# The state operand of a chunked scan, scaled on ScalarE in eight copies in place of one GpSimd product

## The chip, the cores and the metric

The kernel runs on one core of a Trainium2 chip. The metric is the device time of one execution in microseconds (us). The core has five engines that run side by side and meet at semaphores: TensorE (PE in the profile, with its weight loads as PEld), VectorE (DVE), ScalarE (ACT), GpSimd (POOL) and SyncE (SP), which issues the transfers. Each engine takes its own instructions strictly in order.

## The reference

One layer of a Mamba-2 block and a LoRA mixture stand side by side on the same normalised input, and both are added to it. Cut to what matters (L = 2048 positions, 64 heads of width 64, 8 groups of heads, state width 128):

```python
xn = layernorm(x)
proj = xn @ in_proj_w.T                 # gate, (x, B, C) and dt
xBC = silu(causal_conv4(proj[xBC]))
dt_p = softplus(dt + dt_bias); dA = exp(dt_p * -exp(A_log))
def step(state, inp):                   # over the 2048 positions
    state = state * dA_t + (dt_p * x)_t * B_t
    y_t = state . C_t
y = group_norm(y + x * D) * norm_weight * silu(gate)
out = x + y @ out_proj_w.T + ffn(xn)    # ffn: base matmul + top-2 LoRA
```

## The kernel before, in words

All is in float32. The input projection, the output projection and the base matrix are multiplied by Strassen-Winograd schemes with seven products per two-by-two block. In the first part (to about 2690 us) the products of the input projection (`pair`, seven products of eight half-matmuls each) run as a stream of TensorE work, and the scan's small matmuls are set between them. In the last part only the output projection runs.

The step-by-step recurrence is computed in chunks of Q = 128 positions. There are 16 groups-by-halves per 1024 positions, of four chunks each, so 128 slots, one for each chunk of each group of HG = 8 heads. A slot has two halves in the code:

- `scan_a` prepares a chunk, one slot ahead of its use. VectorE's `tensor_tensor_scan` at L688 makes `es`, for each of 8 heads and each of 128 positions the product of decays from a source position to a later one; `es` has one buffer (pool `p1`). TensorE makes C times B and a transpose of B in `ps_cb`, which ScalarE copies out (`cbm` L698, `bt` L700); VectorE multiplies `es` by `cbm` into `dab` (L702). TensorE transposes x into `ps_xt` (L88); ScalarE copies it out head by head, each scaled by its dt, into `xdt` (L713, eight copies of 128x64). Then `xdd` is `xdt` times the decay from each position to the chunk's end, the last column of `es`. `xdd` has one buffer too.
- `scan_b` uses it: eight matmul pairs `ps_y` from `xdt` and `dab`, four pairs `ps_e` from the state and C, VectorE's `ecp` and `y` (L759, L760), then the matmul `ps_st` from `bt` and `xdd` (L764). The state is multiplied by the chunk's whole decay on GpSimd (L769, through the helper `gp`, L83) and `ps_st` is added on VectorE (L774).

What else stands on the engines around it: on GpSimd the sums of weights for the Strassen scheme (`add` in `left_operands`, L427, and `level_one_sums` for the output weights `wo`, through L83); on ScalarE the copy `s1` of product one (L474), stores' functions (L529, L533), the convolution's first tap (L640), its silu (L653), squares (L798) and the norm's root (L809); on VectorE the other taps of the convolution (L646) and the sums that read a product's PSUM (L478, L482, L531). The fourth product of the second PSUM tile (`px`) writes the bank that an L531 has to have read.

The order on each engine is made when the program is recorded: a scheduler places the instructions by its own costs, and those given to `keep_in_program_order` keep the order of the code (the matmuls through `mm`, the `xdt` copies, and GpSimd's products in the second half through `gp`). Transfers all go through SyncE's queue.

Of the kernel before, what the change touches and what calls it, by code (L numbers as in the profile page):

```python
# [9 lines left out]
AF = mybir.ActivationFunctionType  # L10
ALU = mybir.AluOpType
# [5 lines left out]
HP = 64  # L17
G = 8
HG = H // G
# [8 lines left out]
P = 128  # L28
# [3 lines left out]
Q = 128  # L32
# [10 lines left out]
def mamba_lora_kernel(  # L43
# [17 lines left out]
    nc = tc.nc  # L61
# [16 lines left out]
    def mm(*args, **kw):  # L78
        tc.keep_in_program_order(nc.tensor.matmul(*args, **kw))  # L79

    def gp(s, *args):

        ins = nc.gpsimd.tensor_tensor(*args)  # L83
        if s:
            tc.keep_in_program_order(ins)

    def transpose(out, in_):
        tc.keep_in_program_order(nc.tensor.transpose(out, in_, ident))  # L88
# [590 lines left out]
    def scan_a(s, g, half, c):  # L679

        key = s, g, half, c
        n = f"{s}_{g}_{half}_{c}"
        dab, ecp = decay_of.pop(key)
        hs = slice(g * HG, (g + 1) * HG)
        cs = slice(c * Q, (c + 1) * Q)

        es = p1.tile([P, HG, Q], F32, tag="es", name=f"es_{n}")
        nc.vector.tensor_tensor_scan(  # L688
            es.rearrange("p h t -> p (h t)"), dab.rearrange("p h t -> p (h t)"), here, 0.0,
            ALU.mult, ALU.add,  # L690
        )
        yield
        xg, bc = xbc_of[s, g, half]
        psm = ps_one.tile([P, 2, Q], F32, tag="aux", name=f"ps_cb_{n}")
        mm(psm[:, 0, :], bc[:, 0, cs], bc[:, 1, cs], start=True, stop=True)
        transpose(psm[:, 1, :], bc[:, 0, cs])
        cbm = p2.tile([P, Q], F32, tag="cbm", name=f"cbm_{n}")
        nc.scalar.copy(cbm, psm[:, 0, :])  # L698
        bt = p2.tile([P, Q], F32, tag="bt", name=f"bt_{n}")
        nc.scalar.copy(bt, psm[:, 1, :])  # L700
        ms = dab
        nc.vector.tensor_tensor(  # L702
            ms, es, cbm.unsqueeze(1).to_broadcast([P, HG, Q]), ALU.mult
        )
        yield
        pst = ps_one.tile([P, 4, Q], F32, tag="aux", name=f"ps_xt_{n}")
        for j in range(4):
            transpose(pst[:, j, :], xg[:, j, cs])
        xdt = p2.tile([P, HG, HP], F32, tag="xdt", name=f"xdt_{n}")
        x_t = pst.rearrange("p j (a q) -> p (j a) q", q=HP)  # L710
        for h in range(HG):
            at = g * HG + h
            ins = nc.scalar.activation(  # L713
                xdt[:, h, :], x_t[:, h, :], AF.Copy,
                scale=dt_of[s][:, half * NQ + c, at : at + 1],
            )
            tc.keep_in_program_order(ins)

        xdd = p1.tile([P, HG, HP], F32, tag="xdd", name=f"xdd_{n}")
        gp(s, xdd, xdt, es[:, :, Q - 1 : Q].to_broadcast([P, HG, HP]), ALU.mult)  # L720
        mid_of[key] = ms, ecp, bt, xdt, xdd
        yield

# [231 lines left out]
    for _ in scan_a(*blocks[0], 0):  # L955
        pass
# [17 lines left out]
    for b, blk in enumerate(blocks):  # L974
        s, g, half = blk
# [15 lines left out]
        for c in range(NQ):  # L991
# [22 lines left out]
            if b == 1 and c < 2:  # L1014
# [3 lines left out]
                    lambda j=j: nc.sync.dma_start(xop_d[0][j], ops_of["x", 0][j]) for j in js  # L1018
                ]
            a = scan_a(*follow) if follow else iter(())  # L1020
            parts = [side[i * len(side) // n : (i + 1) * len(side) // n] for i in range(n)]

# [376 lines left out]
```

## Time and profile before

| what | value |
|---|---|
| median of 3 runs | 3461.18 us (3456.09 to 3463.89) |
| the profiled execution's own time | 3459.94 us |
| its span | 3458.2 us |
| TensorE busy | 3409.4 us (99%) |
| VectorE busy | 2530.2 us (73%) |
| ScalarE busy | 926.4 us (27%) |
| GpSimd busy | 832.3 us (24%) |
| `xdd` on GpSimd, L83 | 128 instructions, 145.3 us busy |
| `xdt` on ScalarE, L713 | 1024 instructions, 223.2 us busy |

The span is the time from the first to the last instruction of the profiled execution. A group's row gives its busy time, the mean duration of one instruction in ns, and the idle time of its engine just before it with what ended that idle time. TensorE's granted clock is at 0.996 of full speed, so differences are not of the clock. From the start to 180 us the kernel normalises the input and makes the decays; from 180 to about 2690 us the slots run, some 19.7 us each; the rest is the output projection.

### The profile page before, as it was taken

How to read it: one execution, taken by the hardware profiler on the slowest of the kernel's cores; microseconds unless marked ns; L12 is line 12 of the kernel's file. 1: busy time of each engine (PE TensorE's matmuls, PEld its weight loads, DVE VectorE, ACT ScalarE, POOL GpSimd, SP SyncE). 2: the span in 40 equal slices, each digit the busy share in tenths (PEclk: the TensorE clock that was granted, in tenths of full speed). 3: DMA queues.
4: the chain of work that ended last, by engine and by line, in shares of the span. 5: the costliest groups of instructions: out<-in, count | busy, mean ns of one | idle time of the engine just before them, and what ended most of it. 6: DMA issues, size and time to landing. Idle time of an engine off the chain costs nothing.

```text
span 3458.2 us, 37638 instructions
## 1 busy us (share of the span) xinstructions
PE 3409.4 (99%) x12818; PEld 1993.4 (58%) x12818; DVE 2530.2 (73%) x2861; ACT 926.4 (27%) x2158; POOL 832.3 (24%) x571
## 2 busy tenths in 40 slices
PE   9999999999999999999999999999999999999999
PEld 7444544544545554444555555444445588888888
DVE  7548787877887877677888887777885466566665
ACT  2223343333433333323333333333331000000000
POOL 3133323233333211332332433322332000000000
PEclk9999999999999999999999999999999999999999
DMA  6546655655656676787787788787777687585644
GB/s 234 189 164 201 209 178 189 206 191 197 199 193 205 197 262 220 246 283 231 240 251 245 234 260 253 234 255 226 244 233 270 236 279 242 198 299 188 213 165 145
DMA packets 530319, 769.79 MB, mean 223 GB/s; under 512 B 35152, under 2 KB 264656, under 8 KB 527440
## 3 DMA queue, kind: packets, MB, share of 16 engines
q1 hardware_dynamic: 530128, 767.39, 68.6%
q8 instruction: 102, 1.67, 0.2%
q14 instruction: 89, 0.73, 0.1%
HBM read 516.64 MB, written 250.61 MB: 222 GB/s over the span
## 4 chain that ended last, share of the span: by engine, by line
PE 77%; DVE 10%; issue 6%; DMA 4%; POOL 2%; ACT 1%; SPq 0%; POOLq 0%; DVEq 0%; ACTq 0%
PE ps_x_x L79 10%; PE ps_x_w L79 8%; PE ps_a_x L79 7%; PE ps_y_x L79 7%; PE ps_x_g L79 6%; PE ps_a_w L79 6%; PE ps_y_w L79 6%; PE ps_y_g L79 4%; PE ps_a_g L79 4%; PE ps_y L79 3%; PE ps_e L79 3%; PE ps_x_b L79 2%; PE ps_st L79 2%; PE ps_a_b L79 2%; PE ps_y_b L79 2%
## 5 line engine op out<-in xcount | busy, mean ns | idle before, releaser
L688 DVE TENSOR_TENSOR_SCAN es<-dab,here 128x1024 f32<-128x1024 f32 x128 | 327.3, 2557 | 285.8 <-POOL xdd L83 264.6
L83 POOL TENSOR_TENSOR xdd<-xdt,es 128x512 f32<-128x512 f32 x128 | 145.3, 1135 | 1003.4 <-ACT xdt L713 967.6
L646 DVE SCALAR_TENSOR_TENSOR xg<-rawx,cw,xg 128x512 f32<-128x512 f32 x384 | 339.8, 934 | 22.3 <-ACT xg L640 21.7
L79 PE MATMUL ps_x_w<-t,w 128*128 128x256 f32 x1344 | 303.8, 379 | 0.0
L79 PEld LDWEIGHTS ps_x_w<-t,w 128*128 128x128 f32 x1344 | 255.4, 190 | 41.5 <-issue 7.7
L713 ACT ACTIVATE xdt<-ps_xt,dt 128x64 f32<-128x64 f32 x1024 | 223.2, 331 | 201.4 <-PE ps_xt L88 201.4
L83 POOL TENSOR_TENSOR wo<-wo 128x512 f32<-128x512 f32 (+1 forms) x112 | 214.1, 1912 | 16.6 <-DMA ecp<-run_d 10.3
L83 POOL TENSOR_TENSOR state<-state,tot 128x512 f32<-128x512 f32 x112 | 134.5, 1201 | 322.4 <-PE ps_e L79 311.0
L79 PE MATMUL ps_a_w<-q,w 128*128 128x256 f32 x896 | 202.5, 379 | 0.0
L702 DVE TENSOR_TENSOR dab<-es,cbm 128x1024 f32<-128x1024 f32 x128 | 174.1, 1360 | 27.5 <-ACT cbm L698 27.4
L1336 ACT COPY s<-ps_a_w 128x512 f32<-128x512 f32 x28 | 16.4, 585 | 636.2 <-PE ps_a_w L79 568.9
L79 PEld LDWEIGHTS ps_a_w<-q,w 128*128 128x128 f32 x896 | 170.2, 190 | 23.6 <-issue 0.5
L79 PEld LDWEIGHTS ps_y<-dab,xdt 128*64 128x64 f32 x2048 | 114.0, 138 | 109.6 <-issue 72.6
L79 PE MATMUL ps_y_x<-op_again,s_x 128*128 128x512 f32 x384 | 173.3, 594 | 0.0
L79 PE MATMUL ps_x_x<-op_again,s_x 128*128 128x512 f32 x384 | 172.7, 592 | 0.0
L79 PE MATMUL ps_a_x<-op_again,a_x 128*128 128x512 f32 x384 | 172.7, 592 | 0.0
L79 PE MATMUL ps_x_x<-op,s_x 128*128 128x512 f32 x368 | 165.5, 592 | 0.0
L79 PE MATMUL ps_y_x<-op,s_x 128*128 128x512 f32 x368 | 165.5, 592 | 0.0
L79 PE MATMUL ps_a_x<-op,a_x 128*128 128x512 f32 x368 | 165.4, 592 | 0.0
L646 DVE SCALAR_TENSOR_TENSOR bc<-rawb,cw,bc 128x512 f32<-128x512 f32 x192 | 159.1, 859 | 4.0 <-ACT bc L640 3.2
L79 PE MATMUL ps_y<-dab,xdt 128*64 128x128 f32 x2048 | 145.9, 283 | 13.4 <-ACT xdt L713 13.4
L79 PE MATMUL ps_e<-bc,state 128*128 128x128 f32 x960 | 142.1, 292 | 0.0
(236 smaller groups left out, 6050.7 us busy)
## 6 DMA issues: line engine op xcount, KB each, us to landing
w<-w SPq DMA_DIRECT2D x196, 512.0 KB, 3.7
dab<-da_d SPq DMA_DIRECT2D x128, 512.0 KB, 5.1
raw<-ev SPq DMA_DIRECT2D x192, 256.0 KB, 3.2
a_x<-in_w_in_dram SPq DMA_DIRECT2D x168, 256.0 KB, 4.2
w<-wo SPq DMA_DIRECT2D x96, 448.0 KB, 3.5
ecp<-run_d SPq DMA_DIRECT2D x256, 128.0 KB, 4.0
gate<-ev SPq DMA_DIRECT2D x128, 256.0 KB, 3.5
sg<-gate SPq DMA_DIRECT2D x32, 1024.0 KB, 7.3
```

Of the source, the lines that this page charges most:

```text
L79: tc.keep_in_program_order(nc.tensor.matmul(*args, **kw))
L83: ins = nc.gpsimd.tensor_tensor(*args)
L646: nc.vector.scalar_tensor_tensor(dst[:, i, :], raw[:, i, k : k + TB], cw[:, ti, k : k + 1], dst[:, i, :], ALU.mult, ALU.add,)
L688: nc.vector.tensor_tensor_scan(es.rearrange("p h t -> p (h t)"), dab.rearrange("p h t -> p (h t)"), here, 0.0, ALU.mult, ALU.add,)
L702: nc.vector.tensor_tensor(ms, es, cbm.unsqueeze(1).to_broadcast([P, HG, Q]), ALU.mult)
L713: ins = nc.scalar.activation(xdt[:, h, :], x_t[:, h, :], AF.Copy, scale=dt_of[s][:, half * NQ + c, at : at + 1],)
L1336: nc.scalar.copy(s1, pa)
```

## The change

The one GpSimd instruction that multiplied the 128x512 tile `xdt` by the broadcast last column of `es` is replaced by eight ScalarE activations of 128x64, one for each head, with the function Copy and the head's column as the scale. They keep the order of the code behind the eight `xdt` copies. The buffers and what they hold stay as they are.

```diff
         xdd = p1.tile([P, HG, HP], F32, tag="xdd", name=f"xdd_{n}")
-        gp(s, xdd, xdt, es[:, :, Q - 1 : Q].to_broadcast([P, HG, HP]), ALU.mult)
+        for h in range(HG):
+            ins = nc.scalar.activation(
+                xdd[:, h, :], xdt[:, h, :], AF.Copy, scale=es[:, h, Q - 1 : Q]
+            )
+            tc.keep_in_program_order(ins)
         mid_of[key] = ms, ecp, bt, xdt, xdd
         yield
```

## Prediction

> **What bounds the kernel now.** I read the page first (busy times, slices, costliest groups), then TensorE's own list of waits, then what waits for `xdd`, then the stretch of the timeline around the longest such wait.
>
> ```profile
> span 3458.2 us, 37638 instructions
> ...
> PE 3409.4 (99%) x12818; PEld 1993.4 (58%) x12818; DVE 2530.2 (73%) x2861; ACT 926.4 (27%) x2158; POOL 832.3 (24%) x571
> ...
> L688 DVE TENSOR_TENSOR_SCAN es<-dab,here 128x1024 f32<-128x1024 f32 x128 | 327.3, 2557 | 285.8 <-POOL xdd L83 264.6
> L83 POOL TENSOR_TENSOR xdd<-xdt,es 128x512 f32<-128x512 f32 x128 | 145.3, 1135 | 1003.4 <-ACT xdt L713 967.6
> L646 DVE SCALAR_TENSOR_TENSOR xg<-rawx,cw,xg 128x512 f32<-128x512 f32 x384 | 339.8, 934 | 22.3 <-ACT xg L640 21.7
> ...
> L713 ACT ACTIVATE xdt<-ps_xt,dt 128x64 f32<-128x64 f32 x1024 | 223.2, 331 | 201.4 <-PE ps_xt L88 201.4
> ```
>
> TensorE is busy for 3409.4 of 3458.2 us; no other engine passes 73%. So the kernel is bound by TensorE's stream of matmuls, and an edit on other engines is worth only what it takes from, or adds to, the 48.8 us in which TensorE is idle (plus slow matmuls after a stop). GpSimd's 145.3 us on `xdd` and VectorE's 264.6 us of waiting for it look large, but both lie beside that stream. The waits of TensorE tell what can be won:
>
> ```profile
> PE ps_y L79 <- ACT xdt L713: 13.4, 5, 6.8
> PE ps_nv L79 <- ACT xdt L713: 10.0, 4, 2.7
> PE ps_st L79 <- POOL xdd L83: 5.4, 1, 5.4
> ...
> PE ps_x_g L79 <- DVE ev L531: 2.7, 4, 1.3
> ...
> PE ps_x_x L79 <- DVE ev L531: 1.7, 4, 0.6
> ```
>
> Columns: total us, times, longest. In 120 slots with a state matmul, TensorE waited for GpSimd's `xdd` once. That once is here:
>
> ```profile
> 1465.48 1.09 PE L79 MATMUL ps_y<-dab,xdt 128*64 128x128 f32 x16
> 1465.55 1.12 ACT L653 ACTIVATE xg<-xg 128x1024 f32<-128x1024 f32 x1
> 1466.51 1.16 PE L79 MATMUL ps_e<-bc,state 128*128 128x128 f32 x8
> 1466.69 5.29 POOL L83 TENSOR_TENSOR wo<-wo 128x512 f32<-128x512 f32 x4 [10.34 <-DMA ecp<-run_d]
> 1471.94 1.06 POOL L83 TENSOR_TENSOR xdd<-xdt,es 128x512 f32<-128x512 f32 x1
> 1473.03 3.11 DVE L688 TENSOR_TENSOR_SCAN es<-dab,here 128x1024 f32<-128x1024 f32 x1 [6.21 <-POOL xdd L83]
> ```
>
> Four sums of the output weights (5.29 us), late because of a transfer, stand in GpSimd's queue ahead of `xdd`, whose inputs had been ready since 1465.7; `ps_st` starts at 1473.05 after 5.38 us.
>
> **The change part by part.**
>
> *Removed from GpSimd:* 128 products, 145.3 us. The wait above goes: -5.4 us. Behind it the timeline has the two `ps_st` matmuls in 2.07 us (1.02 elsewhere) and six of the next product in 3.37 us, where eight take 3.60, so six take 2.7: another 1.7 us. Together -7.1. The rest of GpSimd's queue (sums of weights L427 and `wo`, `state` L83) no longer stands behind a product that waits 967.6 us for ScalarE. In the built program its order is otherwise unchanged. SyncE's stores of these sums can issue earlier, and in the rebuilt order a few dozen transfers stand some places earlier or later. I cost this at nothing: past the first 10 us no transfer ends a wait of TensorE; if that cover were gone, a wait of a product on an `a_x` or `s_x` load would appear in TensorE's list.
>
> *Added on ScalarE:* 8 x 128 = 1024 copies of 128x64, straight behind the eight `xdt` copies of the slot. No table load is added. Each waits for its own `xdt` copy, eight instructions back and so finished. The nearest row is L713, same shape, Copy with a scale from a pointer: 331 ns each, but a slot's eight take 223.2 / 128 = 1.74 us, since they overlap. They read PSUM, the new ones SBUF, so I check by L640, which reads SBUF: one takes 0.80 us, three 2.23, a spacing of 0.71. The new copies have 448 elements fewer, at 0.90 ns (L529 takes 596 ns for 512, L798 1057 for 1024), which leaves 0.31, and one pointer fewer, worth 0.1 (L640's 805 against L529's 596, two pointers): 0.21 x 7 + 0.35 = 1.8 us. [...] I take 1.8, with 1.74 below and 8 x 331 = 2.65 (no overlap) above. ScalarE's load grows by 128 x 1.8 = 230 us to some 1157, a third of the span.
>
> *On the path, `ps_st`.* `xdd` ended a median 1.13 us behind the last `xdt`; now 1.8. From the starts in the trace, `ps_st` starts 1.41 to 13.25 us behind the end of `xdt`, median 4.4, 10th percentile 3.1: TensorE first does sixteen `ps_y` (1.09) and eight `ps_e` (1.16). [...]
>
> *ScalarE's own queue.* Behind the copies stand, in the next place, L640 (31 slots), L533 (22), L474 (17), L809 (14), L653 (13), L529 (11). For a later `xdt` nothing is lost: between one slot's `xdt` and the next ScalarE is idle for at least 8.2 us. L474, which product two waits for, has 3.9 us or more. What is thin is the start of the convolution: pushing each ScalarE instruction by what idle time does not absorb of 1.8 us, taps L646 on VectorE come late in some 20 places, about 10 us in all. A late tap reaches TensorE only through L531, the PSUM adds queued behind the taps, which product four of the pair waits for. I let a fifth of it through: +2 us (0 to +10).
>
> *Moved on VectorE.* The scan `es` of the next slot overwrites what `xdd` reads. In the built program it now stands one place later in 89 of 127 slots, behind a PSUM add (L531, L478 or L482). [...] The `dab` product behind it keeps at least 2.4 us to its user, median 8.9. [...] In 23 of 251 cases an L531 add ends under 0.2 us before the matmul that waits for it: +2.3 us (0 to +12.2, the sum of shortfalls if every add came 0.5 later). The earlier adds could take away the two L531 rows above, 4.4 us, but at 801.8, 1051.9 and 1619.4 us, three of the longest, the add stands behind a burst of L646, not behind a scan, so 0 (to -4.4).
>
> **Sum.** -7.1 + 1.2 + 2 + 2.3 = -1.6 us. The profiled execution took 3459.94 us (span 3458.2 and 1.7 around it), 1.2 under the median of 3461.18. So the profiled time would be 3458 and the median 3460; by the page's 2.0 us per slot it would be 0.7 more. The three runs shown lie 0.2% apart, about what a measurement of this kernel can tell from no change; 0.2% is 6.9 us.
>
> **The rivals.** *Only the gains count (faster, 0.25).* [...]
>
> *VectorE's bursts slip (slower, 0.32).* [...] It decides once adds at those 23 tight places come 0.5 us later; 1.75 later would be 58.8 us. For it: VectorE is at 7 to 8 tenths through the scan. Against it: by the stages of the windows view it is busy 1942 of the 2510 us from 180 to 2690, and less than half of the idle 568 was the wait for `xdd`.
>
> *It does little (0.43).* Stall and slips nearly cancel, 3460, own range 3455 to 3467.
>
> The range: 3448 takes in most of the first rival, 3482 the second with `ps_st` at its upper price.
>
> **What would show it.** `xdd` as ScalarE rows, 1.7 to 2.65 us for eight; POOL near 687 us; no wait of `ps_st` over a microsecond; `es` waiting far less than 264.6 us, and for ScalarE; L646's mean under 934. I am wrong if `ps_st` waits for ScalarE in more than about ten slots, if rows of L531 in TensorE's list pass 12 us, if `ps_y` waits for `xdt` more often than 5 times, or if a transfer appears there.

## The result, and the profile after

The changed kernel takes 3451.86 us in the median of 13 runs (3450.24 to 3456.24), the kernel before, run beside it, 3459.83 (13 runs, 3455.95 to 3463.89). The ratio is 0.9979, interval [0.9971, 0.9988]: 8 us faster, between 4 and 10. That lies in the predicted range (3448 to 3482) and at the edge of the 0.2% that I had called measurable, but the likeliest number, 3460, missed it by 8 us. The profiled execution took 3453.59 us, 1.7 above its median. In the five series of runs of this document the kernel before has medians from 3457.07 to 3459.83 us, so one or two of the 8 us can be scatter.

The page after, its head and the groups that answer to those shown of before:

```profile
span 3451.8 us, 38274 instructions
...
PE 3409.2 (99%) x12818; PEld 1992.3 (58%) x12818; DVE 2501.2 (72%) x2861; ACT 1164.7 (34%) x3182; POOL 696.1 (20%) x443
...
L688 DVE TENSOR_TENSOR_SCAN es<-dab,here 128x1024 f32<-128x1024 f32 x128 | 304.6, 2380 | 83.4 <-ACT xdd L721 81.8
L646 DVE SCALAR_TENSOR_TENSOR xg<-rawx,cw,xg 128x512 f32<-128x512 f32 x384 | 339.2, 933 | 18.7 <-ACT xg L640 18.0
...
L713 ACT ACTIVATE xdt<-ps_xt,dt 128x64 f32<-128x64 f32 x1024 | 223.8, 333 | 209.7 <-PE ps_xt L88 209.7
...
L721 ACT ACTIVATE xdd<-xdt,es 128x64 f32<-128x64 f32 x1024 | 261.9, 388 | 0.0
```

GpSimd gave up 136 us, ScalarE took on 238, VectorE waits 202 us less before its scans (285.8 to 83.4), and TensorE's busy time is the same to 0.2 us. What moved the end is in TensorE's own list of waits (total us, times, longest):

```profile
PE ps_nv L79 <- ACT xdt L713: 10.5, 4, 3.3
PE ps_y L79 <- ACT xdt L713: 7.8, 5, 4.6
...
PE ps_x_x L79 <- DVE ev L531: 2.8, 3, 1.3
PE ps_x_g L79 <- DVE ev L531: 2.5, 5, 0.9
PE ps_e L79 <- ACT da L346: 1.8, 2, 0.9
PE ps_st L79 <- ACT xdd L721: 1.4, 4, 0.4
```

The stop of 5.4 us behind GpSimd is gone, and in its place stand four waits of 0.4 us or less. A new row is that of `da` (L346), a ScalarE copy of the decays of later positions. TensorE issues the same matmuls in the same order in both kernels, so the two traces can be laid on each other matmul by matmul. The start of each in the trace after, less its start before, steps by -6.8 us over the five matmuls from the stop on (-5.29, -0.48, -0.42, -0.42, -0.21), and is -6.35 us at the end. So in this pair of traces all else sums to +0.5 us.

### The profile page after: what moved, and what is told of

The parts are those of the page before. It is cut to its first block, busy times and chain, and to the rows that moved or that the text cites. A ratio compares the mean times of both kernels' runs of the same rounds, so it can differ in the third digit from the quotient of the medians.

```text
span 3451.8 us, 38274 instructions
## 1 busy us (share of the span) xinstructions
PE 3409.2 (99%) x12818; PEld 1992.3 (58%) x12818; DVE 2501.2 (72%) x2861; ACT 1164.7 (34%) x3182; POOL 696.1 (20%) x443
## 4 chain that ended last, share of the span: by engine, by line
PE 84%; DVE 9%; issue 3%; ACT 2%; DMA 1%; POOL 0%; SPq 0%; DVEq 0%; ACTq 0%; POOLq 0%
PE ps_x_x L79 12%; PE ps_x_w L79 8%; PE ps_a_x L79 8%; PE ps_y_x L79 8%; PE ps_x_g L79 7%; PE ps_a_w L79 6%; PE ps_y_w L79 6%; PE ps_y_g L79 5%; PE ps_a_g L79 4%; PE ps_y L79 3%; PE ps_e L79 3%; PE ps_st L79 2%; PE ps_x_b L79 2%; DVE xg L646 2%; PE ps_a_b L79 2%
## 5 line engine op out<-in xcount | busy, mean ns | idle before, releaser
L83 POOL TENSOR_TENSOR state<-state,tot 128x512 f32<-128x512 f32 x112 | 153.7, 1373 | 1326.0 <-PE ps_e L79 1199.8
L688 DVE TENSOR_TENSOR_SCAN es<-dab,here 128x1024 f32<-128x1024 f32 x128 | 304.6, 2380 | 83.4 <-ACT xdd L721 81.8
L646 DVE SCALAR_TENSOR_TENSOR xg<-rawx,cw,xg 128x512 f32<-128x512 f32 x384 | 339.2, 933 | 18.7 <-ACT xg L640 18.0
L713 ACT ACTIVATE xdt<-ps_xt,dt 128x64 f32<-128x64 f32 x1024 | 223.8, 333 | 209.7 <-PE ps_xt L88 209.7
L721 ACT ACTIVATE xdd<-xdt,es 128x64 f32<-128x64 f32 x1024 | 261.9, 388 | 0.0
L531 DVE TENSOR_TENSOR ev<-ps_x_x,s_x 128x512 f32<-128x512 f32 x94 | 64.5, 687 | 120.5 <-PE ps_x_x L79 116.1
L646 DVE SCALAR_TENSOR_TENSOR bc<-rawb,cw,bc 128x512 f32<-128x512 f32 x192 | 145.7, 790 | 1.9 <-ACT bc L640 1.0
```

The lines of the kernel that those rows point to most:

```text
L531: nc.vector.tensor_tensor(e, ps, add, alu)
L646: nc.vector.scalar_tensor_tensor(dst[:, i, :], raw[:, i, k : k + TB], cw[:, ti, k : k + 1], dst[:, i, :], ALU.mult, ALU.add,)
L688: nc.vector.tensor_tensor_scan(es.rearrange("p h t -> p (h t)"), dab.rearrange("p h t -> p (h t)"), here, 0.0, ALU.mult, ALU.add,)
L713: ins = nc.scalar.activation(xdt[:, h, :], x_t[:, h, :], AF.Copy, scale=dt_of[s][:, half * NQ + c, at : at + 1],)
L721: ins = nc.scalar.activation(xdd[:, h, :], xdt[:, h, :], AF.Copy, scale=es[:, h, Q - 1 : Q])
```

## The experiments

In the expectations, theory A says that the one stop at 1473 us is the gain and the rest cancels. Theory B says that the gain is spread over the slots. Theory C says that VectorE's order, where the scan `es` stands among the PSUM adds, carries it; theory D, that GpSimd's queue does. Line numbers in the lines shown shift by a few with each kernel's edit.

**One slot alone, twice.** The eight ScalarE copies stand only in the slot of the stop (the branch cut out below); the other 127 keep GpSimd's product.

```diff
-        gp(s, xdd, xdt, es[:, :, Q - 1 : Q].to_broadcast([P, HG, HP]), ALU.mult)
+        if key == (0, 7, 1, 2):
...
+        else:
+            gp(s, xdd, xdt, es[:, :, Q - 1 : Q].to_broadcast([P, HG, HP]), ALU.mult)
```

> ScalarE makes xdd in one slot only, the one whose state matmul stopped TensorE for 5.4 us at 1473 us (first half of the positions, last group, second half, third chunk); the other 127 stay on GpSimd. Theory A (the gain is that one stop and the slow matmuls behind it): 6 to 8 us under before, and from 1500 us on a constant lead of about 7 us over before. Theory B (the gain is spread: GpSimd off, VectorE's scan behind an add, earlier adds, slot by slot): within 2 us of before, because a wait elsewhere takes the place of the stop.

It took 3455.47 us against 3457.07, ratio 0.9996 [0.9988, 1.0004], though its trace no longer had the stop. The number is theory B's, and so is the reason that B gave, a wait elsewhere in the place of the stop; that the gain is spread is not shown by it. The profiled execution (3450.91 us) was the fastest of its 13, a poor witness for the median. So it was run again.

> The kernel with the ScalarE copies in the one slot behind the four sums, a second time, since its first median (1.6 us under the kernel before) and its first trace (the stop gone, 6.6 us) do not agree. Theory A (that stop is the gain, 6.5 us, and the first median was low by chance): 3450 to 3453, ratio 0.998 to 0.999. If the ratio is over 0.9992 again, the slot's stop alone is not worth its 6.5 us in most executions, and the trace should show what takes its place: a wait of ps_xt for bt behind it of 2.4 us, as in the first trace.

The median was the same, 3455.48 against 3458.37, ratio 0.9992 [0.9983, 1.0001], above the 3450 to 3453 of theory A, and this time the profiled execution (3456.63 us) lay near it. Here are the lines of TensorE's, VectorE's and SyncE's waits (the last between 1440 and 1485 us), and then of the timeline (start, duration, engine):

```profile
PE ps_xt L88 <- ACT bt L700: 4.3, 2, 3.8
```

```profile
DVE es L688 <- DMA dab<-da_d: 13.6, 3, 11.8
```

```profile
SPq L874 <- POOL wo L83: 8.2, 1, 8.2
```

```profile
1472.62 2.16 SPq L874 DMA_DIRECT2D w<-wo  x3
...
1479.57 0.67 SPq L874 DMA_DIRECT2D w<-wo  x1
...
1480.66 2.37 SPq L665 DMA_DIRECT2D dab<-da_d  x1
...
1491.14 2.29 DVE L688 TENSOR_TENSOR_SCAN es<-dab,here 128x1024 f32<-128x1024 f32 x1 [11.81 <-DMA dab<-da_d]
...
1495.84 2.73 DVE L800 SCALAR_TENSOR_TENSOR xg<-xg,dsk,y 128x512 f32<-128x512 f32 x4
...
1497.28 1.06 ACT L805 ACTIVATE y<-xg 128x1024 f32<-128x1024 f32 x1 [11.13 <-DVE xg L800]
...
1499.57 0.25 ACT L700 COPY bt<-ps_cb 128x128 f32<-128x128 f32 x1
...
1499.87 1.12 PE L88 MATMUL ps_xt<-ident,xg 128*128 128x128 f32 x4 [3.79 <-ACT bt L700]
```

Read it downwards. GpSimd's `wo` sums are as late as before. Their stores `w<-wo` wait for them and hold SyncE's queue for 8.2 us, to 1472.6. The load of the next slot's decays, `dab<-da_d`, stands behind them and needs 10.4 us from issue to landing (2.4 of them in the issue itself), where its median is 5.2. The scan waits 11.8 us for it; `xg` behind it on VectorE, the square on ScalarE and then `bt` come late, and one slot after the removed stop TensorE stops for 3.8 us. Laid on the second trace of before (below), this kernel is 6.6 us earlier behind the old stop and gives 4.0 back by 1600 us; the 2.6 that remain fit the 1.6 and 2.9 us of the two medians. In the first trace of this kernel the scan waited 9.6 us and TensorE 2.4: the later the load, the longer the new stop. In the kernel before, the same load is as late (issued at 1481.14), but there TensorE is held up as well.

Why the whole change does not pay this is seen in its timeline; the second fence is that of the kernel before:

```profile
1428.60 5.32 POOL L83 TENSOR_TENSOR wb<-wb 128x512 f32<-128x512 f32 x4
...
1436.26 2.72 SPq L874 DMA_DIRECT2D wo<-in_w_out_dram  x4
...
1446.61 6.16 POOL L83 TENSOR_TENSOR wo<-wo 128x512 f32<-128x512 f32 x4
...
1471.44 0.51 SPq L665 DMA_DIRECT2D dab<-da_d  x1
```

```profile
1446.60 1.06 POOL L83 TENSOR_TENSOR xdd<-xdt,es 128x512 f32<-128x512 f32 x1 [12.77 <-DMA y<-xg]
1447.62 7.74 POOL L83 TENSOR_TENSOR wb<-wb 128x512 f32<-128x512 f32 x4
...
1457.58 2.73 SPq L870 DMA_DIRECT2D wo<-in_w_out_dram  x4
...
1466.69 5.29 POOL L83 TENSOR_TENSOR wo<-wo 128x512 f32<-128x512 f32 x4 [10.34 <-DMA ecp<-run_d]
...
1481.14 1.99 SPq L665 DMA_DIRECT2D dab<-da_d  x1
```

Before, the sums `wb` of the slot ahead queue behind that slot's product, which waits until 1446.6; then the loads of `wo`, its sums and the decays' load are late in turn. Without a product in that earlier slot the `wb` sums run at 1428.6 and the `wo` sums 20 us earlier (5 of them are the lead that this trace has by then), and the stores no longer hold the load: its longest wait on VectorE is 1.0 us.

**All but that slot.** The complement: GpSimd keeps the product only in the slot of the stop.

```diff
-        if key == (0, 7, 1, 2):
+        if key != (0, 7, 1, 2):
```

> The reverse: ScalarE makes xdd in 127 slots, and in the slot of the 5.4 us stop it stays on GpSimd behind the four sums of output weights. Theory A: within 2 us of before, with the stop of about 5 us back in TensorE's waits for xdd. Theory B: 6 to 8 us under before, like the changed kernel.

It took 3450.61 us against 3457.07, ratio 0.9983 [0.9976, 0.9989]. The stop did not come back: the `wo` sums ran at 1444.7 to 1450.8, and the one GpSimd product, at 1458.75, had nothing in front of it. The number is again theory B's, and theory A's returning stop did not come, but the trace shows why: the product of the slot before was gone too. So the stop has two conditions, the product in its own slot and the late sums of the slot before, and taking either away removes it; only the second also brings the decays' load forward.

**The sums behind the product.** All products stay on GpSimd; in the one slot the first step of the `wo` sums is issued after `xdd`.

```diff
-            if 0 <= b - 15 < 16 and c:
+            if 0 <= b - 15 < 16 and c and (b, c) != (15, 1):
...
+            if (b, c) == (15, 1):
+                next(left_sums)
```

> All of xdd stays on GpSimd; only the first step of the output weights' sums (four adds, 5.3 us) is issued after xdd of that slot rather than ahead of it. No ScalarE copies. Theory A: 6 to 8 us under before: the stop was a place in GpSimd's queue, not the price of the product. Theory B: within 2 us of before.

It took 3451.53 us, ratio 0.9986 [0.9979, 0.9993]: 5.5 us, a little under theory A's 6 to 8 and well over B's 2, with VectorE's scans where they were and still waiting for GpSimd. In its trace the decays' load is late too, a wait of 7.7 us, but the wait of `ps_xt` for `bt` is 0.5 at most, so almost nothing is given back. Its gain and that of the change can't be told apart: the intervals overlap.

**The kernel before once more.**

> The kernel before, unchanged, for a second profile and for the size of chance. Theory A: ratio 1.000, and in the profile the stop of 5 us at 1473 us is there again. If the stop is absent and the span no shorter, the stop was one execution's chance, and the gain must lie elsewhere. Differences between this trace and the first one give the noise of a comparison of two traces: I expect 2 to 4 us.

Ratio 1.000 [0.9991, 1.0009]. The stop is there again, 4.9 us (`ps_st` behind `xdd`, at 1470.78). Against this trace the change gains 6.5 us at the stop and 4.3 at the end. The two traces of before differ by 2.1 us at their ends, and single waits of `ps_y` for `xdt` move by as much: that at 1206 us by 1.4 us between these two, that at 957 us by 2.3 between them and the trace with the sums behind. So one trace against another settles no difference of 2 us.

**No product at all.** `ps_st` reads `xdt` in place of `xdd`: the scaling is left out.

```diff
-        xdd = p1.tile([P, HG, HP], F32, tag="xdd", name=f"xdd_{n}")
-        gp(s, xdd, xdt, es[:, :, Q - 1 : Q].to_broadcast([P, HG, HP]), ALU.mult)
+        xdd = xdt
```

> The product is left out on every engine: the state matmul reads xdt, so the state misses its decay to the chunk's end. Bounds what any way of making xdd can give. Theory A: 7 to 10 us under before, at most 3 us better than the changed kernel, since beside the one stop xdd costs TensorE only about 1.4 us on ScalarE. Theory B: at least 12 us under before, since the load on ScalarE or GpSimd and the scan's wait cost something in each slot.

Less work, and slower: 3468.88 us, ratio 1.0036 [1.0022, 1.0050]. Both theories expected a gain of 7 us or more, and both fail. The stop at 1473 us is gone here too, so other places cost some 16 us more in the trace. With nothing left that reads `es` late, the scheduler put the scans up to nine places earlier on VectorE (one of them 21), ahead of adds and taps. In TensorE's list the L531 rows grew from 5.3 us in the changed kernel to 9.9, and ScalarE's `xdt` is late too:

```profile
PE ps_y L79 <- ACT xdt L713: 16.1, 5, 7.5
PE ps_nv L79 <- ACT xdt L713: 13.2, 4, 3.5
PE ps_x_x L79 <- DVE ev L531: 6.2, 4, 2.1
...
PE ps_x_g L79 <- DVE ev L531: 3.7, 4, 1.5
```

**The order held fixed.** To compare engines in one order, the scan and the PSUM adds of L478, L482 and L531 were kept in the order of the code, with the product on GpSimd, on ScalarE, and with none (there `ps_st` reads `xdt`). The edit is the same in all three, and the same at L482, L531 and the scan L688 as at L478, shown here:

```diff
-        nc.vector.tensor_tensor(s16, px, s1, ALU.add)
+        tc.keep_in_program_order(nc.vector.tensor_tensor(s16, px, s1, ALU.add))
...
```

> xdd on GpSimd as before, but VectorE's scans and PSUM adds are held in the order of the code, which puts each scan some four places later than before, behind the adds and behind ecp, y and state. With the next two kernels it forms a set in which VectorE's order is the same (up to 79 places) and only the maker of xdd differs. Theory C (what decides is where the scan stands in VectorE's queue; the changed kernel gains because its scan stands behind a PSUM add): this kernel and the ScalarE one of the set lie within 3 us of each other. Theory D (GpSimd's queue decides: a product that waits there for ScalarE holds up sums and, through their stores, transfers): this one is 5 to 8 us slower than the ScalarE one. Against before it may go either way, since the scan stands later than in either kernel.

> The changed kernel (eight ScalarE copies) with VectorE's scans and adds held in the order of the code. Theory C: within 3 us of the GpSimd kernel of the set. Theory D: 5 to 8 us under it.

> The set's third: no product at all, the state matmul reads xdt (the state misses its decay to the chunk's end), VectorE's order that of the GpSimd kernel of the set. Without the pinned order the kernel without the product was 12 us slower than before, its scans standing up to nine places earlier. Theory C: that loss was the order, so here it is gone: this kernel is not slower than the other two of the set by more than 2 us, and at most 3 us faster. If leaving the product out costs something by itself, it is 8 us or more slower than they are.

They took 3511.65, 3506.59 and 3490.58 us (ratios 1.0153 [1.0139, 1.0167], 1.0135 [1.0121, 1.0149], 1.0094 [1.0080, 1.0108]). The edit put the scans some four places later, behind `ecp`, `y` and the state's add, so this is not the changed kernel's order. Laid on the trace of before, the first two are 16 and 14 us late by 200 us, before the slots' part of the work is reached, where adds of the first products come late (as in the next pair), and lose another 30 or so in the slots. Three readings stand. The held order costs far more than the engine of `xdd`. Between GpSimd and ScalarE the medians differ by 5 us, with overlapping intervals, and the two profiled executions end level (3505.73 and 3506.05 us): the ScalarE one gains 6.3 us at the stop and loses as much in other places, so this pair decides nothing between C and D. And without a product the kernel is 21 and 16 us faster than the other two, where 3 at most were expected. In one order of VectorE, then, leaving the product out brings time, and the 12 us that it cost above came with the new order. In the traces, 8 us of that gain are two stops of `ps_st` for GpSimd's `xdd` (at 1508 and 1794 us); the rest is in small steps, most of them waits for VectorE's sums.

**The order close to the changed one.** The scan and the PSUM adds keep the order of the code as above, `ecp` (L759) too, and the scan is recorded ahead of `scan_b`. It stands one place later than before in 42 slots with GpSimd and in 72 with ScalarE (89 in the changed kernel), and two or more places later in 27 and 26 (7 in the changed kernel). The cut shows the step that moved:

```diff
+            next(a, None)
...
-            next(a, None)
```

> The product stays on GpSimd; only VectorE's order is brought near the changed kernel's: the scan is recorded ahead of scan_b of its slot and keeps the order of the code with the PSUM adds, so in about half of the slots it stands behind one add that it preceded. Theory A (the gain is the one stop behind the four sums; VectorE's order as changed costs and brings nothing): the stop stays where the weights' transfers are as late as in the kernel before, so 3457 to 3461. Theory C (VectorE's order carries the gain, since adds that end under 0.2 us ahead of their matmul come earlier): 3450 to 3454, with rows of L531 in TensorE's list under 4 us. A rise of 10 us or more would say that even one place behind an add costs, and that the ScalarE copies paid for it.

> As the run beside it, with the eight ScalarE copies; the scan stands one place later in 72 slots, as in the changed kernel in 89. Theory A: 5 to 7 us below its GpSimd twin, the stop of TensorE for GpSimd's product being the whole difference; so 3450 to 3455. Theory C: the same time as the twin within 2 us.

They took 3486.00 and 3475.82 us, ratios 1.0079 [1.0065, 1.0092] and 1.0052 [1.0039, 1.0064], neither near the expected 3450 to 3461. The traces say where: against that of before they are 17.2 and 15.3 us late by 200 us already, where the first products' adds, held in order by the edit, come late. The waits of the GpSimd one:

```profile
PE ps_x_g L79 <- DVE s_g L478: 9.7, 2, 7.7
PE ps_x_x L79 <- DVE s_x L478: 7.1, 1, 7.1
PE ps_st L79 <- POOL xdd L83: 4.9, 1, 4.9
```

The same two rows of L478 stand in the three kernels above. But the pair keeps its worth, 10 us in the medians: between 1400 and 1500 us the ScalarE one gains 6.1 on its twin, where the 4.9 us stop is. 1.9 us lie ahead of 200 us, and the rest in small steps before the stop. That is theory A's prediction of 5 to 7 us in its place, somewhat exceeded in sum, and C's "within 2 us" fails. Behind 200 us the GpSimd one loses another 11 us on the trace of before, and the ScalarE one some 8 beside what it gains at the stop. A rise of 10 us was to mean that one place behind an add costs time; but the adds and `ecp` are held here as well and a fifth of the scans stand further back, so what one place costs stays open.

**The copies doubled.** Each slot writes its eight copies twice.

```diff
-        for h in range(HG):
+        for h in [*range(HG), *range(HG)]:
```

> The eight ScalarE copies are written twice, the second time over the first: 1.9 us more of ScalarE in each slot, xdd ready 3.8 us behind xdt. The prediction's slack for the state matmul (1.4 us at the least, 3.1 at the 10th percentile, 4.4 in the median) says that some 30 slots are now short, together about 25 us. Theory C agrees if VectorE's order (scan one to two places later than before) stays as good: 3470 to 3485 us. If ScalarE's slack is deeper than that, under 3460.

It took 3509.92 us, ratio 1.0145 [1.0131, 1.0159]: 58 us above the changed kernel, where 18 to 33 were expected. The waits alone came to the sum reckoned from the slack of `ps_st`, 25 us, though in 18 slots and not in 30 (the list leaves out waits of 0.15 us or less; there are 34 of these):

```profile
PE ps_st L79 <- ACT xdd L721: 24.0, 18, 2.3
```

But TensorE's busy time rose too, from 3409.2 to 3430.8 us. The timeline of TensorE behind one of those waits shows how (us from the start, duration):

```profile
1230.37 1.12 PE L79 MATMUL ps_st<-xdd,bt 128*128 128x512 f32 x2 [2.26 <-ACT xdd L721]
...
1231.33 5.29 PE L79 MATMUL ps_y_x<-op,s_x 128*128 128x512 f32 x8
```

Eight such matmuls take 3.60 us elsewhere. After a wait of 2.26 us they took 1.7 more: four of them 0.42 late each, in a stretch in which the granted clock is 0.50 (last section). Such stretches hold 8.4 us of the added busy time. Another 12.5 us are in the first matmuls behind TensorE's stops, 82 here and 31 in the changed kernel with the shortest counted: 0.27 us for each, and most of the stops that came new are under 0.15 us long. The added waits of `ps_st` (22.6) and the added busy time (21.6) make 44 of the 58 us; the rest is spread over other waits, such as those behind L531 (5.3 us in the changed kernel, 10.0 here) and of `da` (1.8 and 3.6). VectorE's order moved as well, with 48 scans two or three places later than before, so the rest is not ScalarE's load for certain.

## Why the prediction was right or wrong

*The stop: right in size and place.* I had 5.4 us and 1.7 of slow matmuls, -7.1. Laid on the two traces of before, it is -6.8 and -6.5, and the kernel with the sums moved gains most of the change's 8 us without any ScalarE copy. What I called slow matmuls is a stretch of 3.4 us at half clock (0.50, last section). The mean granted clock of 0.996, from which the differences seemed not to be of the clock, hides it.

*GpSimd's queue and SyncE's, costed at nothing: the figure stood, the reason did not.* I had written that no transfer ends a wait of TensorE, and named a product's `a_x` or `s_x` load as the sign that the cover was gone. The kernel with one slot changed shows that removing the stop alone exposes the decays' load behind the late stores, 4.0 of 6.6 us, through three engines. The change escapes that because every product is gone from GpSimd's queue, so the sums and their stores run 20 us earlier. The zero was two effects, one of which had to cancel the other.

*Eight copies: 1.8 us predicted; the last ends 1.88 behind the last `xdt` in each slot.* Right on the path, but not for the reason given. One takes 388 ns, where L713's takes 333, and the eight are busy for 261.9 / 128 = 2.05 us, 238 ns from start to start. The 1.74 of the nearest row, 197 ns from start to start, whose copies read PSUM, did not carry over to these, which read SBUF. No run of before shows the 2.0 us per slot that stands beside the sum; what the runs showed is these 2.05. The last copy still ends at 1.88 because the first starts 0.16 us before the last `xdt` copy has ended.

*`ps_st`, +1.2: right as a wait, too small as time.* No run shows the 1.2; it was an estimate of mine. The trace after has 1.4 us of waits in 4 slots, and at each of the four places (706.6, 958.5, 1210 and 2521 us in the trace of before) TensorE slips 0.52 us for a wait of 0.4 or less, 2.1 in all.

*Late taps, +2: this did not happen.* L646's wait for L640 fell from 21.7 to 18.0 us. What ScalarE's load did delay is something that I had not listed: the `da` copy behind a slot's copies, 0.95 us of slip at two places (727 and 1230 us).

*VectorE, +2.3: wrong in where, small in sum.* No run shows the 2.3 either; it too was an estimate of mine. I expected L646's mean under 934 ns; on `xg` it is 933. What did get shorter is the scan, 2557 to 2380 ns (22.7 us), and L646 on `bc`, 859 to 790 ns (13.3 us). The tight L531 adds stayed a small cost: 5.3 us of L531 rows in TensorE's list against 4.4, under my bound of 12. Of the three L531 waits that I would not count on, the one at 801.8 us did go (-1.5 us), and a slip of 1.5 us appeared at 1984 us, behind an L531 add.

*The sum.* It was -1.6 and the measured difference is -8, so the step that was off is the +5.5 that I set against the stop. Seven traces can be laid on each other matmul by matmul: before (twice), one slot alone (twice), the sums behind, the changed kernel and all but that slot. A step that stands in both of the last two, with ScalarE's copies in nearly all slots, and in none of the other five is the change. Four such steps are gains that I had put at zero: the wait of `ps_y` for `xdt` at 452 us (4.6 us in place of 6.2 to 6.8), that of `ps_st` for `mean` at 638 us (-0.8), the L531 wait at 801.8 us (-1.5) and a wait at 1137 us (-0.4), together some -4.6 us. The losses are `ps_st` (2.1), `da` (1.9), 1984 us (1.5), and four of 0.4 to 0.5 us at 1585, 1619, 2322 and 2514 us, together some +7.3. So about +2.7 stood in the place of +5.5. With the stop that makes some -4 us, the lower end of the measured 4 to 10. What lies between this and 8 us stays open: the waits at 957, 1052 and 1206 us differ among the five as well, and so do stretches of half clock.

*The rivals.* That the result stands on the side of "only the gains count" is luck. The 4.4 us of L531 rows did not go (5.3 after) and the `ps_nv` waits did not shrink (10.5 us against 10.0); only the late taps stayed away. "VectorE's bursts slip" needed adds late at the 23 tight places; the L531 rows grew by 0.9 us. With the scans some four places later and the adds held, some 30 us are lost in the slots, so the order can cost that much; here one place later in 89 slots did not.

## What to carry to other kernels

When one wait of the bounding engine is removed, look at the queue that made it late: the same lateness may be waiting on a second path, here through SyncE's stores to a load. In the changed kernel it is the absence of a blocking instruction in the slots before, not in the slot of the stop, that kept the gain. And an edit that frees a scheduler (leaving work out, holding an order) must be read with its new order beside it: here leaving out 128 products cost 12 us where the order was free, and brought 16 to 21 us where it was held.

## What the runs showed of the hardware

Behind two stops TensorE lost more than the stop. After 5.38 us of waiting the two `ps_st` matmuls took 2.07 us in place of 1.02, and after 2.26 us of waiting four of the next eight took twice their usual 0.43 us. In both places the granted clock of TensorE had fallen to half (0.50). These are the stretches behind four stops: of 5.38 us in the kernel before, of 3.79 and 2.42 us in the two traces of one slot alone, and of 2.26 us with the copies doubled. The third number from the end of a line is the granted clock.

```profile
1472.80:1476.20 3.40, 3.15 (x4) 1.51 (x5) 3.17 (x2) 0.00 (x0) 3.40 (x3) 0.50 0.98 271
```

```profile
1499.70:1503.10 3.40, 3.23 (x7) 1.92 (x8) 3.40 (x5) 2.60 (x11) 0.19 (x1) 0.50 1.08 369
```

```profile
1494.70:1498.10 3.40, 3.40 (x11) 1.83 (x12) 3.40 (x5) 3.06 (x10) 0.83 (x1) 1.00 1.07 382
```

```profile
1231.60:1235.00 3.40, 3.40 (x5) 1.35 (x4) 3.40 (x5) 1.54 (x3) 0.00 (x0) 0.50 0.77 217
```

So behind a stop of 2.42 us the clock was 1.00, and behind one of 2.26 us 0.50. Between 200 and 2700 us, the fourteen traces of this document have 89 stops of 0.8 to 1.75 us, and no half clock behind any; 83 of 1.75 to 3 us, and half clock behind 38; and 39 longer ones, and half clock behind all. There, in the traces of before and after, it lasted 3.41 us eight times and 6.83 us once. The length of a stop did not settle whether it came: behind the same wait of 2.1 us at 2178 us the clock fell in two of the seven traces laid on each other, and that cost 1.6 us. What else decides it, these runs do not show.

For a plan, at the three of these places where the clock fell, the stop was worth 1.5 to 1.8 us more than the wait row shows; the stop of 2.42 us was worth 0.2 more. In the profile this appears as busy time, not as a wait.
